# A recurrent layer moved beside its input projection, and another order for the first expert mixes of a SwitchHead kernel

## The chip, the cores and the metric

The kernel runs on one core of one Trainium2 chip. The metric is the device time in microseconds of one execution; of several runs the median is given. A profile of one execution stands beside it.

Engine names as the profile has them: PE is TensorE (matrix multiplication; PEld are its weight loads), ACT is ScalarE, DVE is VectorE, POOL is GpSimd, SP is SyncE, which here only issues transfers.

## The reference

Two blocks follow each other, each with a layer norm ahead of it and a residual addition behind it. The batch B is 2, the length T 2048, the width D 256.

```python
# block 1: a recurrent layer over T
xi = einsum('btd,hd->bth', layernorm(x), Wi) + bi
h[t] = tanh(xi[t] + h[t-1] @ Wh.T + bh)          # h[-1] = 0
x = x + h
# block 2: attention with 8 heads of 64, values and outputs from experts (E = 5, 2 chosen)
q, k = n @ Wq, n @ Wk                            # n = layernorm(x)
wv = topk_mask(n @ Ws, 2) * sigmoid(n @ Ws)      # per token, head and expert
v = einsum('bthe,btek->bhtk', wv, einsum('btd,edk->btek', n, Wv))
attn = softmax(q * scale @ k.T) @ v
out = einsum('bthe,bthk,ekd->btd', topk_mask(n @ Wd, 2), attn, Wo)
x = x + out
```

All numbers are float32.

## The kernel before

**The recurrent layer.** Time is cut into 128 segments of 16 steps (`NCH` = S = 16 steps, NS = P = 128 segments), so that one step of all segments of both batch rows is one operation of 256 columns. Chunk c below is step c of every segment. In the preparation (L274 to L332) each chunk is normalized on POOL (`normalize`, L217), transposed on PE (`turn_in`, L297, 4 transposes into a tile `tp` of the pool `ps_t`), copied by ACT (L299), and multiplied by Wi (`project_in`, L306: for each half mc of the outputs two matmuls, kc = 0 and 1, of 256 columns into a tile px of `ps_xi`). ACT writes px with both biases added to xi (L313). Statistics for the norm come in groups from DVE (`measure`, `stats`, `scales`). The order of PE is written out: the transposes of chunk c + 1, then the projection of chunk c.

The recurrence is run twice. Run "a" starts every segment from zero states at step 3 (SKIP = 3) and gives the last state of each segment (`ends`). Run "b" starts each segment with the state in which run a left the segment ahead of it, and keeps all states (`hs`). At the end `compare` looks whether run b's last states agree with those that it started from; if not, a slow path would run (`slow`). In `step` (L355) each batch row b and each output half mc is a separate matmul pair of 128 columns (L365), an addition of xi on DVE (L372) and a tanh on ACT (L373). For a step without earlier states only a tanh is taken (L359). Beside run b the earlier states are transposed back (L394), added to x and sent out as x1d (`add_back`, L400, L401), and the second norm is started.

**PSUM.** [...] In the attention `ps_s` holds two tiles of two banks for scores, and `ps_o` one bank "o" for output products and one bank "d" for denominators. A bank is given to a new tile when the operations that read its earlier tile are done.

**The attention's main loop (L1154).** A unit is one head with one quarter of the queries (512), 64 units in all. A unit takes U_T = 4 steps T, and each step handles two key tiles t = 2T and 2T + 1, each of 128 x 1024 scores. So unit 0 is T = 0 to 3. In a step the engines get, in this order: the scores of both tiles on PE (`scores`, L638); on ACT a copy p of each tile to SBUF (`stage`, L650); on DVE the running maximum (`largest`, L660, at the end of a unit L663 to L666). ACT and DVE never read one score tile at once: in most steps the odd tile goes first to DVE and then to ACT, the even one first to ACT. At T = 0, 4, 8 and so on both are copied first, the row maximum of the unit just ended is transposed (`turn_max`, L679), reduced (`reduce_max`, L684), and later spread to all rows by PE (`spread_max`, L693, `top` L699). LAG = 6: in step T the tiles 2(T - 5) and 2(T - 5) + 1 get their maximum subtracted (`subtract`, L706; the first two of a unit on DVE, the others on POOL), their exp follows on ACT (L709), and in step T + 1 they are multiplied by the values v (`products`, L719, into bank "o"). POOL then adds pairs of tiles by an accumulating transfer (`fold`, L731), and PE sums them (`sums`, L740, into "d").

Everything else is hung into the steps by hand, in the tables `before` (ahead of the products), `between` (ahead of the odd tile's maximum), `first_behind` and `behind` (at the end of the step); `at(table, T, f, ...)` (L973) appends. Each engine works through its own instructions in the order in which they were issued.

**What of this the change touches.** For the first head and batch row the expert values are made inside T = 0 to 5: `first_experts(c)` (L594) for 16 chunks, three in a step, is 16 PE records (L577) into a bank ("d" for odd c, `misc` for even c) and a copy by ACT (L604) into a tile xf that holds four chunks (a part). After the fourth, SP sends the part to DRAM for later heads (L606). `mix(0, part)` then takes the gates of four chunks (L620, a small copy into a `misc` bank) and multiplies xf by them in place (L622); `mix_sum` (L628) sums over the experts into v. The gates come from `gates` (L959), which POOL finishes (L245 to L256). The output products of T = 6 need part 0 of v, those of T = 7 part 1, and so on. The scheduling is in L996 to L999:

```python
for part in range(4):
    if i == 0:
        at(behind, (3, 5, 6, 7)[part], mix, i, part)
        at(behind, (3, 5, 6, 7)[part], mix_sum, i, part)
```

Of the kernel before, what the change touches and what calls it, by code (L numbers as in the profile page):

```python
# [20 lines left out]
def pass_over(  # L21
# [20 lines left out]
    def tile_pool(name, **kw):  # L42
        return tc_pool(name=name + mark, **kw)
# [80 lines left out]
    def misc(shape, nm):  # L124
        return ps_m.tile(shape, F32, tag="m", name=nm)
# [133 lines left out]

    S = NCH  # L260
    NS = P
    NEWTON = 3


# [8 lines left out]

    with tile_pool(name="prep", bufs=3) as pp, tile_pool(  # L274
        name="lna", bufs=3
    ) as lnp, tile_pool(name="ps_xi", bufs=3, space=PSUM) as ps_xi, tile_pool(
        name="ps_t", bufs=3, space=PSUM
    ) as ps_t, tc.manual_schedule():
        norm_of, turned = {}, {}

        def measure(c0, n):
            mv = pp.tile([P, n * B, 2], F32, tag=f"mv{n}", name=f"mva{c0}")
            for c in range(c0, c0 + n):
                for b in range(B):
                    stats(lnp, mv[:, (c - c0) * B + b, :], xt[c][:, b, :], f"a{c}_{b}")
            neg, y = scales(lnp, mv, n * B, f"a{c0}")
            for c in range(c0, c0 + n):
                norm_of[c] = neg, y, (c - c0) * B

        def turn_in(c):  # L290
            neg, y, k = norm_of.pop(c)
            xn = pp.tile([P, B, D], F32, tag="xn", bufs=2, name=f"xn{c}")
            tp = ps_t.tile([P, KC, B, P], F32, tag="tp", name=f"tpa{c}")
            for b in range(B):
                normalize(xn[:, b, :], xt[c][:, b, :], neg, y, k + b)
                for kc in range(KC):
                    nc.tensor.transpose(tp[:, kc, b, :], xn[:, b, kc * P : (kc + 1) * P], ident)  # L297
            turned[c] = pp.tile([P, KC, B, P], F32, tag="xnT", bufs=2, name=f"xnT{c}")
            nc.scalar.copy(turned[c], tp)  # L299

        def project_in(c):
            xnT = turned.pop(c)
            for mc in range(KC):
                px = ps_xi.tile([P, B, P], F32, tag="px", name=f"px{c}_{mc}")
                for kc in range(KC):
                    nc.tensor.matmul(  # L306
                        px.rearrange("p b n -> p (b n)"),
                        lhsT=wi[:, kc, mc * P : (mc + 1) * P],
                        rhs=xnT[:, kc].rearrange("p b n -> p (b n)"),
                        start=kc == 0,  # L310
                        stop=kc == KC - 1,
                    )
                nc.scalar.activation(xi[:, mc, c], px, AF.Identity, bias=bsum[:, mc : mc + 1])  # L313

        groups, c0 = [], 0
        for n in (1, 1, 2, 3, 4, 5):
            groups.append((c0, n))
            c0 += n
        assert c0 == NCH
        measure(*groups.pop(0))  # L320
        nc.vector.tensor_tensor(bsum, bias[:, 0, :], bias[:, 1, :], ALU.add)
        for c in range(NCH):
            while groups and groups[0][0] <= c + 2:
                measure(*groups.pop(0))
            if c == 0:
                turn_in(0)
            if c < 2:
# [14 lines left out]

    TOL = 4 * 2.0**-23
    GC = NCH // 2
    SKIP = 3
# [6 lines left out]

    def step(nm, s, prev, h, ps_h):  # L355
        for b in range(B):
            if prev is None:
                for mc in range(KC):
                    nc.scalar.activation(h[:, mc, b, :], xi[:, mc, s, b, :], AF.Tanh)  # L359
                continue  # L360
            pre = sp.tile([P, KC, NS], F32, tag=f"pre{b}", name=f"pre{nm}_{s}_{b}")
            for mc in range(KC):
                ph = ps_h.tile([P, NS], F32, tag=f"ph{b}_{mc}", name=f"ph{nm}_{s}_{b}_{mc}")
                for kc in range(KC):
                    nc.tensor.matmul(  # L365
                        ph,
                        lhsT=wh[:, kc, mc * P : (mc + 1) * P],
                        rhs=prev(kc, b),
                        start=kc == 0,
                        stop=kc == KC - 1,  # L370
                    )
# [3 lines left out]
    def run(nm, from_zero, keep_states, ps_h, beside=None):  # L375
        prev = None if from_zero else (lambda kc, b: ends[:, kc, b, 0:NS])
        for s in range(SKIP if from_zero else 0, S):
            if keep_states:
                h = hs[:, :, s]
            elif s == S - 1:  # L380
                h = ends[:, :, :, 1:]
            else:
                h = sp.tile([P, KC, B, NS], F32, tag="h", name=f"h{nm}_{s}")
# [132 lines left out]
    with tile_pool(name="ps_h", bufs=1, space=PSUM) as ps_h:  # L516
        if slow:
            nc.gpsimd.memset(hs[:, :, S - 1], 0.0)
            with tc.For_i(0, NS, 1):
                nc.vector.tensor_copy(ends[:, :, :, 1:], hs[:, :, S - 1])  # L520
                run("c", False, True, ps_h)
# [72 lines left out]
    def first_experts(c):  # L594
# [9 lines left out]
        nc.scalar.copy(xq[:, c % 4], pv.rearrange("p e k -> p k e"))  # L604
        if c % 4 == 3:
# [378 lines left out]
    for i, (b, h) in enumerate(heads):  # L984
# [284 lines left out]
```

## Time and profile before

| | |
|---|---|
| median of 3 runs | 1552.19 us (1551.83 to 1552.85) |
| the profiled execution: time / span | 1552.41 us / 1550.6 us |
| busy: PE / DVE / ACT / POOL | 97% / 84% / 80% / 83% of the span |
| preparation up to run a | to 53.1 us |
| run a (PE L365 pha) | 53.1 to 74.7 us |
| run b and second norm | to 121.5 us |
| main loop, T = 0 at 121.5; T = 9 at | 187.6 us |
| expert values (L577 pvf) | 16 groups, 133.4 to 170.4 us |
| L604 ACT, 128x320 | 16 copies of 427 ns |
| L313 ACT, 128x256 with bias | 32 of 474 ns |
| L622 and L628 DVE, 128x1280 | 1486 ns each |
| transfers L606, 640 KB | 2.9 to 4.1 us from issue to landing |

A line of the profile has the line of the kernel, the engine, the operation, what is written and read, the shape, and a count of records; one float32 matmul leaves two records. In a timeline the first two numbers are start and duration in us; in brackets stands how long the engine was idle just before, and what it waited for. Matmuls are pipelined: a group of records lasts some 0.16 us longer than the distance to the next. In a table of stretches each engine has its busy time and its count of instructions.

### The profile page before, as it was taken

The page shows a single profiled execution, that of the slowest core. Times are in us where ns is not written, and L with a number is a line of the kernel's source. Part 1 is how long each engine was busy: PE and PEld are TensorE (multiplying, and loading weights), DVE is VectorE, ACT ScalarE, POOL GpSimd, SP SyncE. Part 2 cuts the span into 40 slices and gives each one's busy share as a digit, 9 for nine tenths or more (in the row PEclk, how much of TensorE's full clock was granted, in tenths as well). Part 3 has the DMA queues.
Part 4 walks back from the last instruction along what each step waited for, and adds up shares of the span by engine and source line. Part 5 has one row for each costly group of instructions (what it writes and reads, how often), then busy time and mean ns, then how long its engine had stood idle before and what let it go on. Part 6 is the DMA issues. An engine that isn't in the chain of part 4 may idle for free.

```text
span 1550.6 us, 42383 instructions
## 1 busy us (share of the span) xinstructions
PE 1506.5 (97%) x18078; PEld 533.0 (34%) x18078; DVE 1301.1 (84%) x1807; ACT 1242.5 (80%) x1585; POOL 1284.3 (83%) x852
## 2 busy tenths in 40 slices
PE   6999899999999999999999999999999999999997
PEld 5994222222233333333223332222222222222234
DVE  7374899999998888888987778999989999999974
ACT  4674688888888888888887678888888888888872
POOL 3154699999999988999998688899999999999980
PEclk9999999999999999999999999999999999999999
DMA  6021478898888887788797677888888888888965
GB/s 177 1 110 32 116 166 196 188 182 183 181 178 185 185 166 163 169 177 177 165 206 165 166 164 173 173 175 180 176 180 179 175 171 174 174 174 173 208 146 135
DMA packets 87127, 254.52 MB, mean 164 GB/s; under 512 B 11792, under 2 KB 31376, under 8 KB 86928
## 3 DMA queue, kind: packets, MB, share of 16 engines
q0 software_dynamic: 43488, 164.65, 58.0%
q1 hardware_dynamic: 41808, 86.46, 17.0%
q8 instruction: 143, 2.34, 0.6%
q10 hardware_dynamic: 1632, 0.61, 0.2%
q14 instruction: 56, 0.46, 0.1%
HBM read 59.79 MB, written 50.33 MB: 71 GB/s over the span
## 4 chain that ended last, share of the span: by engine, by line
PE 65%; DVE 18%; ACT 7%; issue 5%; DMA 2%; POOL 1%; ACTq 0%; SPq 0%; DVEq 0%; POOLq 0%
PE s L638 22%; PE o L719 18%; DVE m L660 10%; ACT p L650 5%; PE d L740 5%; PE pk L144 3%; PE pq L163 3%; DVE pro L785 3%; PE pz L899 2%; PE phb L365 2%; PE px L306 1%; PE pha L365 1%; DMA p<-p 1%; ACT p L709 1%; PE pv L577 1%
## 5 line engine op out<-in xcount | busy, mean ns | idle before, releaser
L706 POOL TENSOR_TENSOR p<-p,top 128x1024 f32<-128x1024 f32 x378 | 1009.6, 2780 | 26.2 <-ACT top L699 25.9
L650 ACT COPY p<-s 128x1024 f32<-128x1024 f32 x512 | 511.8, 1013 | 143.8 <-issue 59.2
L709 ACT ACTIVATE p<-p 128x1024 f32<-128x1024 f32 x512 | 538.9, 1064 | 49.5 <-DVE p L706 40.5
L638 PE MATMUL s<-q,k 64*32 64x512 f32 x4096 | 501.5, 596 | 4.7 <-ACT p L650 2.4
L638 PE MATMUL s<-qs,k 64*32 64x512 f32 x4096 | 501.5, 596 | 3.4 <-ACT p L650 1.6
L719 PE MATMUL o<-p,v 128*32 128x512 f32 x4096 | 491.6, 597 | 3.2 <-DVE os L756 2.3
L660 DVE TENSOR_TENSOR m<-s,m 128x1024 f32<-128x1024 f32 x320 | 390.9, 1222 | 83.4 <-PE s L638 73.9
L731 POOL DMA_DIRECT2D p<-p x254 | 264.6, 1043 | 94.4 <-issue 40.7
L719 PEld LDWEIGHTS o<-p,v 128*32 128x32 f32 x4096 | 111.8, 109 | 303.8 <-issue 156.6
L638 PEld LDWEIGHTS s<-q,k 64*32 64x32 f32 x4096 | 100.6, 105 | 155.8 <-ACT p L650 59.5
L638 PEld LDWEIGHTS s<-qs,k 64*32 64x32 f32 x4096 | 100.7, 105 | 153.9 <-ACT p L650 58.1
L706 DVE TENSOR_TENSOR p<-p,pt 128x1024 f32<-128x1024 f32 x126 | 152.5, 1210 | 0.0
L740 PE MATMUL d<-p,ones 128*32 128x512 f32 x1032 | 136.8, 592 | 0.7 <-DMA p<-p 0.7
L660 DVE TENSOR_TENSOR m<-s,p 128x1024 f32<-128x1024 f32 x64 | 78.3, 1224 | 47.2 <-ACT p L650 46.2
L785 DVE TENSOR_TENSOR pro<-po,mr 128x1280 f32<-128x1280 f32 (+1 forms) x65 | 95.6, 1471 | 2.6
L622 DVE TENSOR_TENSOR xq<-xq,wp 128x1280 f32<-128x1280 f32 x60 | 89.2, 1487 | 2.1
L628 DVE TENSOR_REDUCE v<-xq 128x256 f32<-128x1280 f32 x60 | 88.5, 1476 | 0.0
L163 PE MATMUL pq<-xn2T,wq 128*32 128x512 f32 x512 | 62.2, 598 | 0.0
L740 PEld LDWEIGHTS d<-p,ones 128*32 128x32 f32 x1032 | 34.1, 110 | 80.2 <-issue 76.9
L144 PE MATMUL pk<-xn2T,wk 128*32 128x512 f32 x512 | 61.5, 598 | 0.0
L835 POOL DMA_DIRECT2D yd<-pro x48 | 60.9, 1268 | 0.0
L400 POOL TENSOR_TENSOR x<-x,hvb 128x512 f32<-128x512 f32 x14 | 17.9, 1275 | 45.8 <-ACT hs L373 34.2
(176 smaller groups left out, 1473.2 us busy)
## 6 DMA issues: line engine op xcount, KB each, us to landing
p<-p POOLq DMA_DIRECT2D x254, 512.0 KB, 5.4
xq<-xvd SPq DMA_DIRECT2D x60, 640.0 KB, 4.6
yd<-pro POOLq DMA_DIRECT2D x48, 640.0 KB, 6.4
qs<-q SPq DMA_DIRECT2D x64, 128.0 KB, 4.4
yd<-pro SPq DMA_DIRECT2D x8, 640.0 KB, 6.3
y<-yd SPq DMA_DIRECT2D x8, 640.0 KB, 6.9
x<-in_x SPq DMA_DIRECT2D x16, 256.0 KB, 6.2
x1d<-x SPq DMA_DIRECT2D x16, 256.0 KB, 2.0
```

The costliest lines, as they stand in the source:

```text
L144: nc.tensor.matmul(pk[at_col : at_col + 32], lhsT=wk[:, kc, h * DH + g : h * DH + g + 32], rhs=xc[:, kc, c0 // 2 : (c0 + HC) // 2, o, :], ...
L163: nc.tensor.matmul(pq[at_col : at_col + 32, :], lhsT=wq[:, kc, h * DH + g : h * DH + g + 32], rhs=xn2T[:, kc, b, n * QB : (n + 1) * QB], s ...
L622: nc.vector.tensor_tensor(xq, xq, wp.unsqueeze(2).to_broadcast([P, 4, DH, E]), ALU.mult)
L638: nc.tensor.matmul(ss[g : g + 32, o, :], lhsT=k_of[i][half, c, g : g + 32], rhs=q_of[i, n][o][half, :], start=True, stop=True, tile_positi ...
L650: nc.scalar.copy(p, ss)
L660: nc.vector.tensor_tensor(m, ss, ring[t - 1] if c == 1 else m, ALU.max)
L706: eng.tensor_tensor(p, p, top.unsqueeze(1).to_broadcast([P, 2, QB]), ALU.subtract)
L709: nc.scalar.activation(ring[t], ring[t], AF.Exp)
L719: nc.tensor.matmul(o_of[u][at_col : at_col + 32, :], lhsT=v_of[i][:, 2 * c + o, g : g + 32], rhs=ring[t][:, o, :], start=c == 0, stop=c == ...
L731: nc.gpsimd.dma_start(out=ring[t], in_=ring.pop(t + 1), accum_op=ALU.add)
L740: nc.tensor.matmul(den_of[u][32 * g : 32 * (g + 1), :], lhsT=ones32, rhs=ring[(t, t1)[g // 2]][:, g % 2, :], start=first, stop=last, tile_ ...
L785: nc.vector.tensor_tensor(dst, po[:, s : s + n, 0:DH].unsqueeze(1).to_broadcast([P, E, n, DH]), mr[:, s : s + n].rearrange("p s e -> p e s ...
```

## The change

Three things are changed, all in `pass_over`.

1. Run a is taken into the preparation. The new `first_run(c)` is called for chunk c - 1 after the projection of chunk c. From step 4 on it multiplies the states of the step before by Wh and accumulates into the px tile that already holds the projection, both batch rows in one matmul of 256 columns; the tanh reads px and adds the biases. For this px tiles have a bank each, six in all, the transposes' tile `tp` moves into the two `misc` banks, and `run` and `step` lose the case of zero states.
2. The expert values of the first head rotate over three banks, `misc`, "o" and "d", instead of two.
3. The mixes of the first head go to T = 2, 4, 5, 6, and their sums to T = 2, 4, 6, 8; mix 1, sum 1 and sum 3 stand in `between`, the others in `behind`.

```diff
-    ) as lnp, tile_pool(name="ps_xi", bufs=3, space=PSUM) as ps_xi, tile_pool(
-        name="ps_t", bufs=3, space=PSUM
-    ) as ps_t, tc.manual_schedule():
-        norm_of, turned = {}, {}
+    ) as lnp, tile_pool(name="ps_xi", bufs=6, space=PSUM) as ps_xi, tc.manual_schedule():
+        norm_of, turned, px_of, h_of = {}, {}, {}, {}
...
-            tp = ps_t.tile([P, KC, B, P], F32, tag="tp", name=f"tpa{c}")
+            tp = misc([P, KC, B, P], f"tpa{c}")
...
         def project_in(c):
             xnT = turned.pop(c)
+            px_of[c] = []
             for mc in range(KC):
-                px = ps_xi.tile([P, B, P], F32, tag="px", name=f"px{c}_{mc}")
+
+                px = ps_xi.tile([P, 512], F32, tag="px", name=f"px{c}_{mc}")[:, : B * P]
...
+                px = px.rearrange("p (b n) -> p b n", b=B)
                 nc.scalar.activation(xi[:, mc, c], px, AF.Identity, bias=bsum[:, mc : mc + 1])
+                px_of[c].append(px)
+
+        def first_run(c):
+
+            pxs, prev = px_of.pop(c), h_of.pop(c - 1, None)
+            if slow or c < SKIP:
+                return
+            h = ends[:, :, :, 1:]
+            if c < S - 1:
+                h = pp.tile([P, KC, B, NS], F32, tag="h", bufs=2, name=f"ha_{c}")
+            for mc, px in enumerate(pxs):
+                for kc in range(KC if prev is not None else 0):
+                    nc.tensor.matmul(
+                        px,
+                        lhsT=wh[:, kc, mc * P : (mc + 1) * P],
+                        rhs=prev[:, kc],
+                        start=False,
+                        stop=kc == KC - 1,
+                        skip_group_check=True,
+                    )
+                nc.scalar.activation(h[:, mc], px, AF.Tanh, bias=bsum[:, mc : mc + 1])
+            h_of[c] = h
...
             if c >= 2:
                 project_in(c)
+            if c:
+                first_run(c - 1)
+        first_run(NCH - 1)
...
-            if prev is None:
-                for mc in range(KC):
-                    nc.scalar.activation(h[:, mc, b, :], xi[:, mc, s, b, :], AF.Tanh)
-                continue
...
-                run("a", True, False, ps_h)
-                run("b", False, True, ps_h, beside)
+                run("b", ps_h, beside)
...
-        pv = ps_o.tile([P, E, DH], F32, tag="d", name=f"pvf{c}") if c % 2 else misc([P, E, DH], f"pvf{c}")
+        tag = (None, "o", "d")[c % 3]
+        pv = ps_o.tile([P, E, DH], F32, tag=tag, name=f"pvf{c}") if tag else misc([P, E, DH], f"pvf{c}")
...
             if i == 0:
-                at(behind, (3, 5, 6, 7)[part], mix, i, part)
-                at(behind, (3, 5, 6, 7)[part], mix_sum, i, part)
+                at(between if part == 1 else behind, (2, 4, 5, 6)[part], mix, i, part)
+                at(between if part % 2 else behind, (2, 4, 6, 8)[part], mix_sum, i, part)
```

More of the change, by code (lines that the diff above doesn't have):

```diff
@@ L261, in pass_over @@
     NS = P
+    SKIP = 3
     NEWTON = 3
@@ L302, in project_in @@
             xnT = turned.pop(c)
+            px_of[c] = []
             for mc in range(KC):
-                px = ps_xi.tile([P, B, P], F32, tag="px", name=f"px{c}_{mc}")
+                px = ps_xi.tile([P, 512], F32, tag="px", name=f"px{c}_{mc}")[:, : B * P]
                 for kc in range(KC):
                     nc.tensor.matmul(
-                        px.rearrange("p b n -> p (b n)"),
+                        px,
                         lhsT=wi[:, kc, mc * P : (mc + 1) * P],
@@ L312, in project_in @@
                     )
+                px = px.rearrange("p (b n) -> p b n", b=B)
                 nc.scalar.activation(xi[:, mc, c], px, AF.Identity, bias=bsum[:, mc : mc + 1])
+                px_of[c].append(px)
[9 more added lines that the diff above has]
+                    nc.tensor.matmul(
+                        px,
+                        lhsT=wh[:, kc, mc * P : (mc + 1) * P],
[6 more added lines that the diff above has]
+            h_of[c] = h
         groups, c0 = [], 0
@@ L332, in pass_over @@
                 project_in(c)
+            if c:
+                first_run(c - 1)
+        first_run(NCH - 1)
     TOL = 4 * 2.0**-23
     GC = NCH // 2
-    SKIP = 3
     sp = rw.enter_context(tile_pool(name="step", bufs=3))
@@ L373, in step, with run @@
                 nc.scalar.activation(h[:, mc, b, :], pre[:, mc, :], AF.Tanh)
[L375 to L383, printed above, removed]
+    def run(nm, ps_h, beside=None):
+        prev = lambda kc, b: ends[:, kc, b, 0:NS]
+        for s in range(S):
+            h = hs[:, :, s]
             step(nm, s, prev, h, ps_h)
@@ L520, in pass_over @@
                 nc.vector.tensor_copy(ends[:, :, :, 1:], hs[:, :, S - 1])
-                run("c", False, True, ps_h)
+                run("c", ps_h)
             for c in range(S):
```

## The prediction

> **What bounds the kernel now.** I read the stages first: the busy time of each engine in stretches that I set by the steps T of the main loop.
>
> ```profile
> core 0: us, PE busy (x) PEld busy (x) DVE busy (x) ACT busy (x) POOL busy (x), PEclk, DMA share, GB/s
> 24.33:53.11 28.78, 27.94 (x151) 24.11 (x151) 11.86 (x58) 19.52 (x40) 11.94 (x22) 1.00 0.05 10
> 53.11:74.65 21.54, 21.54 (x192) 21.54 (x193) 13.68 (x47) 14.81 (x49) 0.00 (x0) 1.00 0.01 2
> 141.80:150.00 8.20, 7.12 (x100) 2.34 (x96) 3.53 (x6) 4.53 (x8) 7.54 (x14) 1.00 0.34 112
> 163.30:170.40 7.10, 5.48 (x92) 1.87 (x92) 5.04 (x6) 4.15 (x6) 4.46 (x2) 1.00 0.23 92
> 180.90:187.60 6.70, 5.01 (x57) 1.75 (x57) 6.35 (x11) 4.98 (x6) 6.62 (x6) 1.00 0.53 131
> 187.60:208.00 20.40, 20.40 (x245) 6.01 (x252) 17.01 (x19) 18.03 (x21) 20.24 (x17) 1.00 0.71 151
> 250.00:400.00 150.00, 149.33 (x1749) 42.45 (x1737) 142.96 (x179) 129.20 (x147) 136.89 (x81) 1.00 0.87 188
> ```
>
> TensorE is the bound nearly everywhere. It is full in the projection (24 to 53) and in the run from zero states (53 to 75), and from 187.6 on it idles under 1%. So a lead that TensorE has at 187.6 should last to the end. Only T = 2 to 8 of the main loop leave it room. The timeline of TensorE shows where (columns: start, duration, idle time before and what ended it).
>
> ```profile
> 146.66 3.44 PE L577 MATMUL pvf<-wv,xn2T 128*32 128x320 f32 x48 [1.08 <-ACT q L173]
> 154.73 1.28 PE L577 MATMUL pvf<-wv,xn2T 128*32 128x320 f32 x16 [0.47 <-ACT xf L604]
> 159.36 0.62 PE L693 MATMUL pt<-ident,mq 128*128 128x128 f32 x4 [0.87 <-DVE mq L684]
> 169.14 1.28 PE L577 MATMUL pvf<-wv,xn2T 128*32 128x320 f32 x16 [1.62 <-ACT xf L604]
> 180.90 0.63 PE L638 MATMUL s<-q,k 64*32 64x512 f32 x4 [1.30 <-ACT p L650]
> 183.38 0.63 PE L679 MATMUL pm<-ident,mm 128*128 128x128 f32 x4 [0.53 <-DVE wp L620]
> 187.02 0.65 PE L693 MATMUL pt<-ident,mq 128*128 128x128 f32 x4 [1.16 <-DVE mq L684]
> ```
>
> These waits are 7.03 us in sum. The first, second and fourth are for a PSUM bank of an expert product; the rest follow VectorE, which does the mixes late (T = 3, 5, 6, 7) and stood still before:
>
> ```profile
> 152.08 1.23 DVE L660 TENSOR_TENSOR m<-s,m 128x1024 f32<-128x1024 f32 x1 [3.96 <-PE s L638]
> 165.33 1.23 DVE L660 TENSOR_TENSOR m<-s,m 128x1024 f32<-128x1024 f32 x1 [4.99 <-PE s L638]
> ```
>
> Last, the timeline where the projection hands over to the run:
>
> ```profile
> 48.73 3.62 PE L306 MATMUL px<-xnT,wi 128*128 128x256 f32 x16
> 52.38 0.47 ACT L313 ACTIVATE xi<-px,bsum 128x256 f32<-128x256 f32 x1 [0.39 <-PE px L306]
> 52.76 0.89 ACT L359 ACTIVATE ha<-xi 128x128 f32<-128x128 f32 x4
> 53.11 17.13 PE L365 MATMUL pha<-ha,wh 128*128 128x128 f32 x151 [0.76 <-ACT ha L359]
> ```
>
> **The run beside the projection.** Before: the chain gives 8 records of px 1.733 us, so the px work is issued by 48.73 + 16 x 0.2166 = 52.20, and run b's first matmul is at 74.65: 22.45 us, of which 192 records take 21.54 (112.2 ns each). After: 12 steps of 8 records of 256 columns, 96 x 0.2166 = 20.79. [...]
>
> Each step needs the tanh of the step before. Its latency: 0.16 drain (a group of 8 lasts 1.89, the next follows after 1.73), 0.03 to ScalarE, 0.474 (L313's form, for L359's 0.30 each), 0.04 back: 0.70. Four transposes (0.44 in the chain) and the next projection (1.73) lie between, 2.17 us: covered. Without them a step would stand 0.70 less 0.43, its first matmul, which needs half the tanh only. That happens once, at step 15: 0.27. Run b then waits 0.70 less 0.22: 0.48. Sum 20.79 + 0.27 + 0.48 = 21.54: **0.9 saved**. ScalarE gets 2 x 0.474 more per chunk, 2.5 us of the 3.9 that TensorE needs, so it hides. The matmul into a bank that ScalarE has read waits for a read that is an iteration old. The 48 additions that VectorE loses (0.29 each) and the transposes' move into two shared banks lie beside TensorE: nothing. Run b's own steps don't change. Bounds for this part: a gain of 1.6 (no waits at the ends) and a loss of 1 (a small wait, 0.15, in each of 12 steps; no row shows one in this pattern).
>
> **Expert values and mixes.** I carried the queues forward with the durations of the rows: scores 1.88, three expert groups 3.37, first copy p 1.2 after the scores start, maximum of the odd tile 2.05 after, mix 0.2 + 1.49, sum 1.49.
> - T = 2: the first product takes the output bank and doesn't wait for the copy of q (1.08, with the restart 1.25). Scores of T = 3 at 148.77 instead of 150.02. Mix 0 and its sum run on VectorE from 148.1 to 151.3, in the 3.96 gap; the gates that it needs were written by 146.9 (L256). The maximum behind them could start at 150.83, so it is 0.46 late.
> - T = 3: no wait for a bank, 154.02 instead of 155.94. Mix 0 is gone from here.
> - T = 4: mix 1 and its sum stand in front of the odd tile's maximum, 157.2 to 160.4. Behind them: that maximum (ends 161.6), then the score bank of T = 5 (needed 162.3), and the last expert product's bank (needed 160.1, free 158.9). Mix 1 overwrites what the transfer of part 1 reads. SP issues it at 153.9; four such landed in 2.9 to 4.1 us, so 156.8 to 158.0: nothing to 0.6 late on VectorE, nothing on TensorE. Scores at 161.36 instead of 163.28.
> - T = 5: the three products follow each other, 163.23 + 3.37: scores of T = 6 at 166.60 instead of 170.35. VectorE: maximum of tile 11 to 164.6, subtraction 0 to 165.8, maximum of tile 10 to 166.9, subtraction 1 to 168.0, mix 2 alone to 169.6.
> - T = 6: scores, keys and output products (1.88 + 1.74 + 1.83) bring TensorE to 172.05 instead of 175.80. VectorE: two maxima to 171.95, sum 2, mix 3 to 175.0; part 3 landed by 172.2 (SP issues it at 168.0).
> - T = 7: the odd maximum ends at 176.2, the copy p behind it frees the score bank at 177.2: scores of T = 8 at 177.26 instead of 180.90. What is late is still VectorE, by mix 3.
> - T = 8: the row maximum comes at 179.8 right after its transposes, as no mix stands ahead of it; its spread follows the output products at 181.5, and T = 9 starts at 182.10 instead of 187.60. Sum 3 stands behind the row maximum, ahead of the odd maximum, whose bank is needed at 183.05 and free at 183.1.
>
> TensorE is 5.5 ahead there. GpSimd isn't. Its first accumulating transfer (175.66) needs the products of T = 6 and comes 3.75 earlier, the second needs exp of tile 3 through the products of T = 7 and comes 3.4 earlier; from then on it is full (20.24 of 20.40 us). The exp of tile 15 starts at 208.07, its subtraction has ended by 206.65: 1.4 of slack. A lead over 3.4 + 1.4 = 4.8 can't pass. Later it has room again (136.89 of 150). **4.8 saved.** Bounds: 5.5 (GpSimd never decides), and 1.25, the first wait alone.
>
> **Sum.** 0.9 + 4.8 = 5.7, from the profiled execution's 1552.41 (span 1550.6 and 1.8 around it): 1546.7; the median of the runs is 0.2 lower: 1546.5.
>
> **Rivals.** (1) GpSimd's pace decides without slack: 0.9 + 3.4 = 4.3, 1547.9. For it: 20.24 of 20.40 busy. Against: it waits for VectorE's comparisons of the gates at 215. (2) The time comes back as other waits, since VectorE does the same work: of 180.9 to 187.6 it was busy 6.35 of 6.70. Then only the first bank's wait and the 0.9 remain: 2.1, 1550.1. Against: the two gaps of 3.96 and 4.99. (3) Slower: mix 1 at T = 4 waits for its transfer, and with it the maximum, the score bank and the expert bank. From a landing later than 158.0 TensorE pays one for one; the whole gain is spent at 163.7, 9.8 us after issue; at 12 us the time is 1554.4. Against: landings of 2.9 to 4.1, and a DMA share of 0.34 and less in these stretches. (4) The tanh isn't covered and each of 11 steps stands 0.27: 3.0 less, 1549.5.
>
> **Chances.** Forecast 0.55 (1545 to 1549), (1) 0.15, (2) and (4) 0.18, (3) and what is like it 0.12, of which about half lies beyond 1555.3. A measurement of this kernel tells about 0.2%, 3.1 us, from no change. Faster: the forecast and two thirds of (1), 0.65; slower by more than that, 0.07; between, 0.28. The range from 1545.0 (0.9 and 5.5 and a little) to 1551.5 leaves out most of (3) and the forecast's edge.
>
> **What would show it.** The last px matmul later than 52.2 by about 17 us but run b's first at 73.3, with one idle of some 0.3 and one of 0.5 us; VectorE's mix at 147 to 151; no TensorE wait for L604; scores of T = 9 about 6.4 earlier in all; exp of tile 15 waiting for GpSimd. I am wrong if idle time in front of L365's new twin comes in every step, if L622 waits for a DMA, or if the lead at T = 9 is gone by 250.

## The result and the profile after

The changed kernel takes 1547.38 us (median of 8 runs, 1546.12 to 1549.05), the kernel before 1552.15 on the same chip: a ratio of 0.9969, interval 0.9958 to 0.998. The forecast was 1546.5, range 1545.0 to 1551.5. Its profiled execution took 1548.75 us (span 1546.9). A later execution of the same kernel, also profiled (`e11_after` below), took 1546.76 (span 1544.9). The largest difference between the two lies at the very start. TensorE's granted clock there, over 24 to 27 us, was 0.53 in the first and 1.00 in the second, so I read the steps from both.

Lines are shifted in the changed kernel: px L307, the new step of run a L328 with its tanh L336, run b L387, expert products L593, mix L637 to L645, scores L655, copy p L667, subtraction L723, exp L726, products L736, fold L748, the closing of a chunk of outputs L791 to L802.

The busy times by stage, first profiled execution (T = 2, 5 and 8 are the third to fifth rows):

```profile
core 0: us, PE busy (x) PEld busy (x) DVE busy (x) ACT busy (x) POOL busy (x), PEclk, DMA share, GB/s
24.36:27.85 3.49, 3.49 (x11) 2.75 (x11) 3.15 (x16) 1.06 (x2) 1.73 (x4) 0.54 0.35 68
27.85:75.09 47.24, 46.54 (x237) 40.35 (x235) 8.83 (x41) 30.05 (x62) 9.77 (x18) 1.00 0.00 1
142.32:149.28 6.96, 6.96 (x101) 2.46 (x97) 4.02 (x8) 4.41 (x8) 6.44 (x12) 1.00 0.37 127
161.79:167.03 5.24, 5.24 (x84) 1.95 (x80) 3.44 (x4) 3.26 (x4) 4.50 (x2) 1.00 0.30 125
177.78:182.68 4.90, 4.90 (x57) 1.74 (x57) 4.39 (x9) 4.90 (x6) 4.82 (x4) 1.00 0.76 193
182.68:203.30 20.62, 20.62 (x245) 5.89 (x252) 17.45 (x19) 18.15 (x22) 20.54 (x18) 1.00 0.67 131
250.00:400.00 150.00, 149.36 (x1756) 42.72 (x1756) 142.95 (x184) 130.42 (x150) 137.26 (x80) 1.00 0.87 185
```

T = 2, 5 and 8 took 8.20, 7.10 and 6.70 us before and take 6.96, 5.24 and 4.90 now, with TensorE full in each. The loss is in the last but one row: GpSimd, 20.54 of 20.62. And one row is new, the first: the granted clock was 0.54 while chunk 3 was projected.

TensorE's timeline at the seam between run a and run b:

```profile
68.78 1.89 PE L307 MATMUL px<-xnT,wi 128*128 128x256 f32 x8
70.51 4.02 PE L328 MATMUL px<-ha,wh 128*128 128x256 f32 x16
75.09 2.05 PE L387 MATMUL phb<-ends,wh 128*128 128x128 f32 x16 [0.56 <-ACT ends L336]
```

The run of L328 lies directly behind the projection of L307, with no idle time until the last step. From VectorE's timeline, the same execution:

```profile
148.82 0.18 DVE L637 COPY wp<-gates_all 128x20 f32<-128x20 f32 x1
149.03 1.49 DVE L639 TENSOR_TENSOR xf<-xf,wp 128x1280 f32<-128x1280 f32 x1
150.55 1.49 DVE L645 TENSOR_REDUCE v<-xf 128x256 f32<-128x1280 f32 x1
...
157.10 0.69 DVE L701 TENSOR_REDUCE mq<-pm 128x4 f32<-128x512 f32 x1 [1.80 <-PE pm L696]
157.70 0.17 DVE L637 COPY wp<-gates_all 128x20 f32<-128x20 f32 x1
157.91 1.49 DVE L639 TENSOR_TENSOR xf<-xf,wp 128x1280 f32<-128x1280 f32 x1
```

Mix 0 fills the gap in which VectorE stood for 3.96 us before. Mix 1 doesn't wait for its transfer, but by little: the trace has it issued at 154.57 and landed at 157.49, and the multiplication that overwrites the tile starts at 157.91.

How far the scores of a step start earlier than before, in us, both counted from the kernel's own T = 0:

| T | forecast | changed kernel | parts 2, 3 | part 2 | part 3 |
|---|---|---|---|---|---|
| 3 | 1.25 | 1.29 | 1.29 | 1.29 | 0 |
| 4 | 1.92 | 1.96 | 1.96 | 1.96 | 0 |
| 5 | 1.92 | 2.03 | 2.02 | 1.21 | -1.02 |
| 6 | 3.75 | 3.86 | 3.86 | 3.04 | -1.02 |
| 7 | 3.75 | 3.86 | 3.86 | 1.70 | -1.02 |
| 8 | 3.64 | 3.66 | 3.67 | 1.21 | -0.32 |
| 9 | 5.50 | 5.46 | 5.46 | 1.21 | 1.48 |
| 13 | - | 5.29 | 5.29 | 1.20 | 1.31 |
| 14 | 4.8 (after tile 15) | 4.35 | 4.33 | 1.22 | -0.55 |
| 24 | 4.8 | 4.34 | 4.35 | 1.21 | -1.37 |

### The profile page after: what moved, and what is told of

The parts are those of the page before. It is cut to its first block, busy times and chain, and to the rows that moved or that the text cites. A ratio compares the mean times of both kernels' runs of the same rounds, so it can differ in the third digit from the quotient of the medians.

```text
span 1546.9 us, 42111 instructions
## 1 busy us (share of the span) xinstructions
PE 1505.9 (97%) x17982; PEld 531.0 (34%) x17982; DVE 1287.2 (83%) x1759; ACT 1238.0 (80%) x1559; POOL 1283.5 (83%) x852
## 3 DMA queue, kind: packets, MB, share of 16 engines
q8 instruction: 143, 2.34, 0.6%
## 4 chain that ended last, share of the span: by engine, by line
PE 66%; DVE 18%; ACT 7%; issue 4%; DMA 1%; POOL 1%; ACTq 0%; DVEq 0%; POOLq 0%
PE s L655 23%; PE o L736 18%; DVE m L677 10%; ACT p L667 5%; PE d L757 4%; PE pq L163 4%; PE pk L144 3%; DVE pro L802 3%; PE pz L916 2%; PE phb L387 2%; PE px L307 2%; DMA p<-p 1%; PE px L328 1%; PE pv L593 1%; ACT p L726 1%
## 5 line engine op out<-in xcount | busy, mean ns | idle before, releaser
L723 POOL TENSOR_TENSOR p<-p,top 128x1024 f32<-128x1024 f32 x378 | 1009.4, 2780 | 24.3 <-ACT top L716 24.0
L667 ACT COPY p<-s 128x1024 f32<-128x1024 f32 x512 | 511.5, 1012 | 143.4 <-issue 59.9
L726 ACT ACTIVATE p<-p 128x1024 f32<-128x1024 f32 x512 | 538.9, 1064 | 50.1 <-DVE p L723 40.7
L655 PE MATMUL s<-q,k 64*32 64x512 f32 x4096 | 501.6, 596 | 4.9 <-ACT p L667 2.5
L655 PE MATMUL s<-qs,k 64*32 64x512 f32 x4096 | 501.7, 596 | 4.3 <-ACT p L667 2.5
L736 PE MATMUL o<-p,v 128*32 128x512 f32 x4096 | 491.6, 597 | 3.2 <-DVE os L773 2.3
L748 POOL DMA_DIRECT2D p<-p x254 | 264.7, 1043 | 91.9 <-issue 40.0
L736 PEld LDWEIGHTS o<-p,v 128*32 128x32 f32 x4096 | 111.8, 109 | 303.7 <-issue 155.9
L655 PEld LDWEIGHTS s<-q,k 64*32 64x32 f32 x4096 | 100.6, 105 | 156.1 <-ACT p L667 59.5
L655 PEld LDWEIGHTS s<-qs,k 64*32 64x32 f32 x4096 | 100.6, 105 | 154.7 <-ACT p L667 60.3
L723 DVE TENSOR_TENSOR p<-p,pt 128x1024 f32<-128x1024 f32 x126 | 152.4, 1210 | 0.0
L802 DVE TENSOR_TENSOR pro<-po,mr 128x1280 f32<-128x1280 f32 (+1 forms) x65 | 95.6, 1471 | 2.6
L645 DVE TENSOR_REDUCE v<-xq 128x256 f32<-128x1280 f32 x60 | 88.6, 1476 | 0.0
L394 DVE TENSOR_TENSOR preb<-phb,xi 128x128 f32<-128x128 f32 x64 | 17.9, 289 | 45.2 <-PE phb L387 45.0
```

The costliest lines, as they stand in the source:

```text
L655: nc.tensor.matmul(ss[g : g + 32, o, :], lhsT=k_of[i][half, c, g : g + 32], rhs=q_of[i, n][o][half, :], start=True, stop=True, tile_positi ...
L667: nc.scalar.copy(p, ss)
L723: eng.tensor_tensor(p, p, top.unsqueeze(1).to_broadcast([P, 2, QB]), ALU.subtract)
L726: nc.scalar.activation(ring[t], ring[t], AF.Exp)
L736: nc.tensor.matmul(o_of[u][at_col : at_col + 32, :], lhsT=v_of[i][:, 2 * c + o, g : g + 32], rhs=ring[t][:, o, :], start=c == 0, stop=c == ...
L748: nc.gpsimd.dma_start(out=ring[t], in_=ring.pop(t + 1), accum_op=ALU.add)
```

## The experiments

My theory after the result had four points. The run beside the projection saves 0.9. The lead at T = 9 needs the banks and the steps together. GpSimd takes back a part, through the output gates and not through the exp that I had named. The spread of the changed kernel's times is the clock at chunk 3. The rivals stand in each expectation. Kernels measured side by side shared a chip and the runs of the kernel before; the ratios are to those. Executions of one kernel lie 4 us apart and more (6.0 in e10_mix1), so a difference of medians under 1 us is read from the traces and not from the medians.

**Each part alone.** `e1_run` has `first_run` and its pools, with the banks and steps of before; `e2_banks_steps` the other two parts; `e3_banks` and `e4_steps` one of these each:

```diff
# e3_banks
-        pv = ps_o.tile(..., tag="d", ...) if c % 2 else misc(...)
+        tag = (None, "o", "d")[c % 3]
+        pv = ps_o.tile(..., tag=tag, ...) if tag else misc(...)
# e4_steps
-                at(behind, (3, 5, 6, 7)[part], mix, i, part)
-                at(behind, (3, 5, 6, 7)[part], mix_sum, i, part)
+                at(between if part == 1 else behind, (2, 4, 5, 6)[part], mix, i, part)
+                at(between if part % 2 else behind, (2, 4, 6, 8)[part], mix_sum, i, part)
```

> Part 1 of the change alone: the run from zero states beside the projection, with the pools and the steps of the mixes as before. Theory: the run takes 96 matmul records of 216.6 ns beside the projection and two waits of about 0.3 and 0.5 us at its end, so from the end of the third chunk's projection to run b's first matmul 47.2 us in place of 48.1: 0.9 us are saved and kept to the end, about 1551.3 us, in executions whose clock holds at 1.0. In executions that take TensorE at half its clock for chunk 3 (the trace of the changed kernel shows 3.49 us for 8 records in place of 1.89), 0.8 slower than that minimum saving allows: about 1552.9. So a median between 1551.3 and 1552.9, and two groups of times some 1.6 to 2.2 us apart. Rival 1: the tanh of one step is not covered, 0.27 us at each of 11 steps: 2.1 us slower than before, 1554.3. Rival 2: nothing is gained, since the attention starts no earlier: 1552.2 in one group.

> Parts 2 and 3 alone: expert values over three banks and the new steps of the mixes, with the run from zero states as its own stage. Theory: the lead of the scores over the kernel before is 5.5 us at T=9 and falls to about 4.3 at T=14, where the closing of the first chunk on VectorE waits for its output gates on GpSimd; it stays there: 4.3 to 5.2 less at the end, about 1547.4 us, and one group of times, since the preparation is that of the kernel before. Rival (the forecast's own cap): the lead after T=15 is 4.8 and nothing on VectorE waits for the gates. Rival 2: the gain needs part 1, lead under 3 us.

> Part 2 alone: expert values over three banks, with the mixes at T=3, 5, 6 and 7 as before. Theory, carried by hand through the first ten chunks: TensorE's waits for the copies of the expert values go, lead of the scores 1.25 us at T=3, 1.9 at T=4 and T=5, 3.75 at T=6, but then the mixes of T=5 to T=7, two steps of VectorE each, stand on the path and give it back: 2.35 at T=7, 1.75 at T=8, 1.5 at T=9; the time is 1.5 us less, about 1550.7. Rival: the lead of T=6, 3.75, holds to the end (the mixes lie beside TensorE): about 1548.4. Rival 2: the banks are worth nothing alone: 1552.2.

> Part 3 alone: the mixes at T=2, 4, 5 and 6 and their sums at T=2, 4, 6 and 8, with the expert values in two banks as before. Theory: TensorE's waits for the copies of the expert values stay, so no lead at T=3 to T=7; VectorE's steps taken apart give 0.75 us at T=8 and 2.6 at T=9, but GpSimd's first folds come no earlier, so that the wait for GpSimd at tile 15 leaves 1.0: about 1551.2 us. Rival: the 2.6 hold to the end, 1549.6. Rival 2: mix 1 a step earlier is late for its transfer, which lands at 157 to 158, and the time rises by 1 or more, 1553.2.

Against the kernel before (1552.50, 40 runs): e1_run 1551.84, ratio 0.9997 (0.9988 to 1.0005). e2_banks_steps 1548.82, 0.9979 (0.9970 to 0.9988). e3_banks 1551.67, 0.9994 (0.9985 to 1.0002). e4_steps 1552.56, 1.0001 (0.9993 to 1.0010).

In the trace of e1_run the start of chunk 3's last px record and run b's first matmul lie 47.62 us apart, in that of before 48.49: 0.87 saved, and the attention behind it is as before to 0.03 us up to T = 40. Its median can't show that. Its times (1550.12 to 1554.43) form no two groups; that part of the expectation failed. e2_banks_steps has the leads of the changed kernel to 0.02 us through T = 24, so up to there part 1 and the others add. Its times were expected in one group near 1547.4, since its preparation is that of before; they lie between 1546.82 and 1550.94, and its trace has the lowered clock at chunk 3 too (0.50 over 26 to 28 us).

Parts 2 and 3 don't add. At T = 14 they have 1.22 and -0.55 alone, together 4.33. With the banks alone, mix 0 with its sum still stands in front of the row maximum, and TensorE's wait for that grows from 0.87 to 1.60, which I hadn't counted when I carried 1.9 for T = 5; the later mixes then hold the copies p. TensorE in e3_banks:

```profile
159.53 0.65 PE L694 MATMUL pt<-ident,mq 128*128 128x128 f32 x4 [1.60 <-DVE mq L685]
175.51 0.63 PE L639 MATMUL s<-qs,k 64*32 64x512 f32 x4 [1.27 <-ACT p L651]
181.11 0.63 PE L639 MATMUL s<-q,k 64*32 64x512 f32 x4 [1.78 <-ACT p L651]
```

With the steps alone both old waits for a bank are there, and a new one between them. TensorE in e4_steps:

```profile
154.67 1.28 PE L577 MATMUL pvf<-wv,xn2T 128*32 128x320 f32 x16 [0.47 <-ACT xf L604]
160.87 3.44 PE L577 MATMUL pvf<-wv,xn2T 128*32 128x320 f32 x48 [1.01 <-DVE xf L622]
170.10 1.28 PE L577 MATMUL pvf<-wv,xn2T 128*32 128x320 f32 x16 [1.62 <-ACT xf L604]
```

The 1.01 is the small copy of gates in front of mix 1. It lies in a `misc` bank, the multiplication on VectorE reads it until 160.82, and the expert product of T = 4 wants that bank. I hadn't counted this tenant, so the lead that I had carried by hand for T = 5, none, was 1.0 off. Over three banks the first product of T = 4 takes bank "o" instead. GpSimd's folds are then 1.0 later as well, the closing of chunk 0 on VectorE waits 1.98 us for its gates, and the lead falls to -0.55 at T = 14, where 1.0 was expected to be left. (The further 0.8 between T = 14 and T = 24 is a stretch at half the clock, from about 214.4 to 217.8 us by the granted clock of 0.80 over 212 to 216 and of 0.77 over 216 to 220. It follows a wait of 1.88 us that TensorE has ahead of T = 14.)

**The fillers.** `e5_fill` puts four unread matmuls into TensorE's idle ahead of chunk 3:

```diff
+            if c == 3:
+                fill = misc([P, 512], "fill")[:, : B * P]
+                for k in range(4):
+                    nc.tensor.matmul(fill, lhsT=wi[:, 0, 0:P], rhs=turned[3][:, 0]..., start=True, stop=True)
             if c + 1 < NCH:
                 turn_in(c + 1)
```

> The changed kernel with four more matmuls of 128x256 on TensorE ahead of chunk 3's projection, which multiply an input already there into a bank that nobody reads, so that TensorE's idle of 1.9 us at 21.5 to 23.5 us is about half filled. They change nothing in what is computed. Theory: the half clock of chunk 3 follows that idle, so the eight records of its projection take 1.9 us in the profiled run (1.5 from the first start to the last) and not 3.5, scores of T=0 start at about 120.5 to 121, and the times lie closer together: the slow half of the changed kernel's executions goes, median some 0.5 to 1 less, about 1546.4. Rival: the granted clock follows its own course, the eight records are at half clock in some executions as before, and the median is that of the changed kernel within 0.5; if the fillers get in the way of chunk 4's transposes, 0.9 slower.

It took 1546.10 us (1545.80 to 1546.99, 5 runs), 0.9964 of before (0.9950 to 0.9977), chunk 3 at full clock (1.00 over 24 to 28 us). For more executions of both I ran the changed kernel and the filled one again side by side:

> The changed kernel itself once more, beside the one with the fillers on the same chip. Theory (the half clock of chunk 3 follows TensorE's idle at 21.5 to 23.5): its executions fall into two groups some 1.6 us apart, as in the first measurement (1546.1 to 1546.7 and 1548.1 to 1549.1), with a third to a half in the upper one. Rival: the spread comes from elsewhere, and it is the same for both kernels.

> The changed kernel with the four fillers once more, beside the changed kernel on the same chip, for more executions of it; the fillers change nothing in what is computed. Theory: no execution has the half clock at chunk 3, so the upper group is missing, the spread is under 1.5 us and the median is 0.5 to 1 below the changed kernel's. Rival: the spread is the changed kernel's, 3 us or more, and the medians agree within 0.4; then the half clock isn't set by that idle.

e11_after 1546.75 (1546.19 to 1549.18, 6 runs), e12_fill 1546.44 (1545.83 to 1547.51, 5 runs), ratios 0.9967 (0.9955 to 0.9979) and 0.9965 (0.9951 to 0.9978). The medians agree within 0.4, as the rival said. The spread with the fillers is 1.7 us, over the 1.5 of the theory and under the 3 of the rival, and of e11_after one execution of six lies in the upper group. Of 14 executions of the changed kernel 5 took over 1548 us, of 10 with the fillers none: with one rate for both that would come out about 1 time in 20. So the times alone don't settle it.

The traces do. Of the 14 profiled executions shown in this document, TensorE stood for 1.9 us ahead of chunk 3's projection in 8, and 4 of these have the lowered clock there (over 26 to 28 us 0.60 in the first execution of the changed kernel, 0.50 in e2_banks_steps, 0.55 in e3_banks, 0.50 in e10_mix1); it stood for 0.6 or less in 6, three with the fillers and three without, and none of these has it (1.00). TensorE at chunk 3 in the first profiled execution of the changed kernel, and then in e11_after:

```profile
23.47 1.10 PE L296 MATMUL tpa<-ident,xn 128*128 128x128 f32 x4 [1.91 <-POOL xn L217]
24.36 3.49 PE L307 MATMUL px<-xnT,wi 128*128 128x256 f32 x8
```

```profile
23.76 0.97 PE L296 MATMUL tpa<-ident,xn 128*128 128x128 f32 x4 [1.91 <-POOL xn L217]
24.57 1.89 PE L307 MATMUL px<-xnT,wi 128*128 128x256 f32 x8
```

The same kernel, and an idle of 1.91 us ahead of these transposes in both; then 3.49 us in one and 1.89 in the other. What differs is when the idle comes. In the first execution the granted clock is recorded at full from 13.94 us, at 0.50 from 24.18, at full again from 27.59 and at 0.50 from 1543.11, behind the last matmul: 3, 4 and 448 times the 3.413 us of that low stretch after the first of these. In the trace of before it is recorded at full from 15.42 us and at 0.50 from 1548.01, behind the last matmul, 449 such stretches later. In e11_after the first rise is recorded at 15.97. At chunk 3 the clock stays low for 3.4 us in all four executions, by its means in windows of 2 us. Laid on stretches of 3.41 us from the first rise, here are the one with the idle and the next in the first execution, and then the two over which the idle falls in e11_after (columns as in the table by stage above):

```profile
20.77:24.18 3.41, 1.40 (x8) 0.74 (x7) 3.00 (x17) 0.91 (x2) 1.32 (x3) 1.00 1.21 205
24.18:27.59 3.41, 3.41 (x10) 2.77 (x10) 3.10 (x16) 1.06 (x2) 1.91 (x4) 0.50 0.42 80
```

```profile
19.38:22.80 3.42, 2.37 (x12) 1.61 (x10) 2.94 (x17) 1.88 (x4) 0.24 (x1) 1.00 1.18 270
22.80:26.21 3.41, 2.36 (x12) 1.94 (x13) 3.21 (x14) 1.06 (x2) 3.06 (x6) 1.00 0.66 120
```

In the first the idle lies in one stretch, of which TensorE was busy for 0.41; in the second it is split, and each half has 0.69. Counted so up to the last matmul, no other stretch of the first execution has less than 0.56, and none of before less than 0.50; before's own idle of 1.91 us is split too (1.72 us busy of the 3.41 from 22.25), and neither trace has another fall of the clock up to there. So in these three executions the lowered clock came where the idle fell into one stretch and not where it was split, and the stretches begin at other times in two executions of the same kernel. For the other executions with this idle that is my reading; it was not shown.

**The output gates.** `e6_gates` makes the output gates of chunks 0 to 7 at T = 3:

```diff
-        at(behind, 7 + 6 * part, gates, 0, part, 1, False)
-        for k in range(E):
-            at(behind, 8 + 6 * part + k, gates_go_on)
+        if part:
+            at(behind, 7 + 6 * part, gates, 0, part, 1, False)
+            for k in range(E):
+                at(behind, 8 + 6 * part + k, gates_go_on)
...
+    at(behind, 3, gates, 0, 0, 1, True)
```

> The changed kernel with the output gates of chunks 0 to 7 made at once at T=3 instead of spread over T=7 to T=12: the same instructions on GpSimd, some 5.5 us of them, ahead of its first subtractions and not between its folds. Theory: GpSimd works without a pause from its first fold at 172 to the end of the gates at 204.6, and that is what the closing of chunk 0 at T=13 waits for; with the gates out of that stretch the closing waits for nothing, and the lead of T=13 (5.3 us, counted from each kernel's own T=0) is kept at T=14 and after, where the changed kernel has 4.35. Some 0.9 us less than the changed kernel at the end. Cost that goes against it: the first subtractions may start 1 us later, at 160.3 in place of 159.2, which has 6 us before the first fold. Rival: the lead after T=14 stays at 4.35, since exp of tile 15 waits for GpSimd's folds and subtractions and not for the gates; then nothing is gained.

1546.24 us (1545.67 to 1548.24, 5 runs), 0.9966 (0.9952 to 0.9979). The lead is 5.30 at T = 13 and still 5.30 at T = 14, 5.34 at T = 24. VectorE at the closing of chunk 0, in the changed kernel and then in e6_gates:

```profile
203.37 0.19 DVE L795 RECIPROCAL po<-den 128x4 f32<-128x4 f32 x1
204.61 0.18 DVE L798 TENSOR_TENSOR mr<-po,gates_all 128x20 f32<-128x20 f32 x1 [1.05 <-POOL gates_all L251]
```

```profile
201.38 0.19 DVE L795 RECIPROCAL po<-den 128x4 f32<-128x4 f32 x1
201.67 0.18 DVE L798 TENSOR_TENSOR mr<-po,gates_all 128x20 f32<-128x20 f32 x1
```

The wait of 1.05 is gone and 0.95 of lead is kept: the theory held. Exp of tile 15, which I had taken for the place, waited 0.17 in the changed kernel (203.61, for GpSimd's L723), and not at all here.

**Mix 3 a step later** (with the gates as in e6_gates): `(2, 4, 5, 6)[part]` becomes `(2, 4, 5, 7)[part]`.

> As the run with the output gates of chunks 0 to 7 made at T=3, and with mix 3 behind T=7 in place of T=6. Theory: at T=8 the scores wait 1.49 us for a copy that VectorE's mix 3 has put off; a step later this lies beside TensorE's work, so the lead grows by 0.5 to 1 us from T=8 on (5.9 to 6.4 at T=9 counted from each kernel's own T=0, where the changed kernel has 5.46) and with the gates out of GpSimd's way it is kept. Rival 1: the mix then stands on the path at T=8 or T=9 and the lead is unchanged at 5.3 by T=10. Rival 2: GpSimd's folds are next, and the lead at T=14 falls back to 4.3.

1546.56 us (1544.43 to 1547.77, 6 runs), 0.9965 (0.9953 to 0.9977). Scores of T = 8 waited for the copy p of T = 7; in the changed kernel and then in e8_mix3:

```profile
177.78 0.63 PE L655 MATMUL s<-q,k 64*32 64x512 f32 x4 [1.49 <-ACT p L667]
```

```profile
175.07 0.63 PE L655 MATMUL s<-q,k 64*32 64x512 f32 x4 [0.57 <-ACT p L667]
```

0.92 less, and the lead is 6.37 at T = 9, 6.21 at T = 14 and 6.23 at T = 24: kept whole up to there. The median doesn't show it, being 0.3 above that of e6_gates.

**Two steps of run a in a row.** In `e7_pairs` first_run is called for two chunks after every second projection:

```diff
-            if c:
+            if c and c % 2 == 0:
+                first_run(c - 2)
                 first_run(c - 1)
+        first_run(NCH - 2)
         first_run(NCH - 1)
```

> The changed kernel with two steps of the run from zero states placed one behind the other after every second chunk's projection, so that in each pair the second step has no projection between it and the tanh it needs. Theory: the tanh of the first of a pair is then in the open, as at the end of the changed kernel's stage, 0.29 us of TensorE idle each time, in 6 to 7 pairs: from the end of chunk 3's projection to run b's first matmul 1.5 to 2 us more than the changed kernel's 47.7 (from start to start), which is more than the 0.87 that the change saved there. Rival: the steps' two halves overlap by themselves and the distance stays at 47.7.

1549.26 us (1547.71 to 1551.65, 20 runs), 0.9982 (0.9976 to 0.9989). From chunk 3's last px to run b 49.86 us instead of 47.61: 2.25 more. TensorE's weight loads show where:

```profile
43.62 1.16 PEld L328 LDWEIGHTS px<-ha,wh 128*128 128x128 f32 x6 [0.51 <-ACT ha L336]
...
51.80 1.16 PEld L328 LDWEIGHTS px<-ha,wh 128*128 128x128 f32 x6 [0.51 <-ACT ha L336]
```

Five pairs (second steps 5, 7, 9, 11, 13) are in the open that were covered, 0.45 us each; I had expected 0.29 in six or seven. The cover was worth more than the whole of part 1.

**Mix 1 a place earlier.** `e10_mix1` brings on the slower rival of the forecast: `at(behind, (2, 3, 5, 6)[part], mix, i, part)`.

> The changed kernel with mix 1 behind T=3, one place ahead of where the change has it. Its values leave for memory at 154.6 and land at 157.5 in the trace of the changed kernel, where the multiplication that overwrites their tile begins at 157.9, 0.4 us later; VectorE is done with the maxima of T=3 at 155.3. Theory (the slower rival of the forecast, brought on by 2.6 us): VectorE waits some 2 us for the transfer, the row maximum mq queued behind it ends 1.9 us later, TensorE waits for it with pt at T=4, and the scores of T=5 start some 1.9 us later than in the changed kernel, counted from T=0; kept to the end, about 1549 us for 1547.4. Rival: the wait lies in VectorE's slack of 1.8 us before mq, and nothing changes.

1550.51 us (1548.24 to 1554.28, 11 runs), 0.9987 (0.9978 to 0.9996). VectorE:

```profile
155.53 0.18 DVE L637 COPY wp<-gates_all 128x20 f32<-128x20 f32 x1
157.81 1.49 DVE L639 TENSOR_TENSOR xf<-xf,wp 128x1280 f32<-128x1280 f32 x1 [2.10 <-DMA xvd<-xf]
159.22 0.68 DVE L701 TENSOR_REDUCE mq<-pm 128x4 f32<-128x512 f32 x1
```

It waits 2.10 us for the transfer, the row maximum queued behind it comes late, and TensorE's `pt` waits 2.7 us for that instead of 0.79. The lead of T = 5 is 0.12, of T = 14 2.41: 1.9 less from there on, as expected. The mechanism of the rival is real, and the change misses it by 0.4 us.

**All that helped together**, `e9_all` (gates, mix 3, fillers):

> The changed kernel with all three: four more matmuls on TensorE ahead of chunk 3's projection (their result is read by nobody), the output gates of chunks 0 to 7 at T=3, and mix 3 behind T=7. Theory: they add up, since each acts at another place: T=0 at about 120.3 with the full clock at chunk 3, 1.9 us more lead at T=14 than the changed kernel; about 1544.3 us, no run with a clock under 0.999, and the times within 1.5 us of each other. Rival: the half clock comes in spite of the fillers, in a third to half of the executions, and the median is near that of the run with the gates and mix 3 alone (1546.6 in the call before, where half its runs were at 0.997).

1545.50 us (1544.97 to 1547.22, 5 runs), 0.9954 (0.9940 to 0.9968). Lead 6.38 at T = 9 and 6.22 at T = 14. That is 1.9 us more than the changed kernel has in the traces, and it holds to T = 121 (6.48, where the changed kernel has 4.49 and 4.61); the intervals of the two ratios still overlap. The expected time was 1.2 lower, and a mean clock of 0.998 in three of its runs was not expected. A part of the 1.9 goes later: at T = 255 the lead is 6.4, and 5.2 and 6.0 in the two executions of the changed kernel. Steps T = 162 and T = 250 last 0.2 us longer in the three traces with the gates moved and in no other, and T = 126 (6.73 in e9_all, 6.00 and 6.58 in the changed kernel) differs from execution to execution.

## Why the prediction was right, step by step

**The run beside the projection, forecast 0.9.** Measured 0.87 or 0.88 in the seven traces that have this stage as the change has it and a full clock. TensorE's chain in the first execution:

```profile
63.33 1.73 PE px L328 x8
65.05 0.44 PE tpa L296 x4
65.49 1.73 PE px L307 x8
67.22 1.73 PE px L328 x8
...
72.44 0.48 ACT ha L336
...
72.96 1.58 PE px L328 x6
...
74.56 0.48 ACT ends L336
...
75.09 0.94 PE phb L387 x6
```

Eight records in 1.73 us, no wait in any step: rival 4 is refuted. The wait at step 15, forecast 0.27, was 0.40: 16 records from 70.67 should have been issued by 70.67 + 16 x 0.2166 = 74.14 and were by 74.54. The wait of run b, forecast 0.48, was 0.55. Together they are 0.2 over the forecast, and yet the total came out, which was luck: the kernel before lost 0.26 at a place that I hadn't counted. In the row below four of its transposes waited between the second and the third and took 0.86 us, where the others take 0.60; in e11_after all of them take 0.60.

```profile
30.71 0.86 PE L297 MATMUL tpa<-ident,xn 128*128 128x128 f32 x4
```

e7_pairs agrees with the larger price, 0.45 for 0.27. My latency of 0.70 was near; what was off is how much of it the first half's matmuls cover.

**TensorE's waits in T = 2 to 8.** The table above: the largest miss is 0.11 us, at T = 5, 6 and 7. The carried queues were right to the place: no wait for a bank is left, and the wait at T = 8 (1.49) is for mix 3. One more wait remains, 0.79 at T = 4 for the row maximum, where before had 0.87.

**"A lead over 3.4 + 1.4 = 4.8 can't pass."** The mechanism held, GpSimd full from its first fold to 204, but both terms were off, and the slack stood at the wrong reader. GpSimd in the changed kernel:

```profile
172.34 1.06 POOL L748 DMA_DIRECT2D p<-p  x1 [6.06 <-ACT p L667]
...
176.01 1.06 POOL L748 DMA_DIRECT2D p<-p  x1
...
198.07 5.51 POOL L723 TENSOR_TENSOR p<-p,top 128x1024 f32<-128x1024 f32 x2
202.79 1.78 POOL L251 TENSOR_SCALAR gates_all<-rank 128x320 f32<-128x320 f32 x1
```

The same in the kernel before, and VectorE at its closing of chunk 0:

```profile
179.33 1.05 POOL L731 DMA_DIRECT2D p<-p  x1
...
201.92 5.19 POOL L706 TENSOR_TENSOR p<-p,top 128x1024 f32<-128x1024 f32 x2
206.65 1.46 POOL L251 TENSOR_SCALAR gates_all<-rank 128x320 f32<-128x320 f32 x1
```

```profile
208.42 0.18 DVE L781 TENSOR_TENSOR mr<-po,gates_all 128x20 f32<-128x20 f32 x1
```

Both folds come 3.86 earlier than before, counted from T = 0 (the second at 179.33 before: 179.33 - 176.01 + 0.54). The gates end at 204.57, before they ended at 208.11, so 4.08 earlier. The closing on VectorE took them up at 208.42 before, 0.31 after their end; in the changed kernel it took them up 0.04 after, so 0.27 of that was slack. 4.08 + 0.27 = 4.35, which is the lead at T = 14. I had looked for the slack only at the exp that I had in mind, and not at each reader of what GpSimd makes in that stretch. The exp's own 1.4 was too long as well: I took the start of the next row (206.65) for the end of the subtractions, which by their own row ran to 201.92 + 5.19 = 207.11. That leaves 0.96, and exp of tile 15 does come 5.0 earlier in the changed kernel (208.07 - 203.61 + 0.54).

**The sum, 5.7.** Of e11_after, at full clock: T = 0 is 0.87 earlier than before, T = 14 is 5.25. Three steps later in the loop (T = 122, 126 and 140) were 0.43, 0.37 and 0.35 shorter than before's. The last addition is 6.9 earlier. The last store then landed 3.94 us after its issue, before 2.98, and the time is 1552.41 - 1546.76 = 5.65 less. So the forecast's 5.7 was met with a smaller gain at T = 14 and two items that I didn't forecast and that nearly cancel: that it came out to 0.05 is luck.

Of the three steps, T = 122 goes with part 1 (5.55 to 5.72 us in the ten traces that have it, 6.04 to 6.77 in the four without), T = 126 lasts 5.50 to 6.82 in no order of the kernels, and T = 140 lasts 7.6 in before and e3_banks and 7.2 in the other twelve. The last store goes with part 1 too. It lands 2.91 to 4.08 us after its issue over the 14 traces, of which the issuing instruction on SyncE makes 1.46 to 1.70 in the four without part 1 and 1.85 to 2.64 in the ten with it, and two executions of one kernel agree (2.34 and 2.51 in the changed kernel, 1.85 and 1.94 with the fillers). So with part 1 the end is later by up to 1.2 us, which can take back the whole 0.87. Why part 1 should change a step and a store so far behind it stays open.

In the first profiled execution chunk 3 at half clock costs 1.6 more (3.49 for 1.89 us), which is most of what separates its 3.66 us from the 5.65. I take it for the reason that the median lies 0.9 over the forecast, between executions near 1546.4 and others near 1548.6; it is shown for this one execution only. (Of the first 8 executions the four over 1548 have a mean clock of 0.997 to 0.998 and the four under it 0.999 to 1.000; in e11_after one of 1546.19 has 0.998 too.) It was no step of mine. The profile of before showed PEclk 1.00 in that stretch.

**The rivals.** GpSimd without slack (1547.9): nearest in size, half right, since the slack was 0.27 and not nil, but on a lead of 4.08. The time coming back as other waits (1550.1): not here, but it is what happens to part 2 or part 3 alone. Slower by the transfer of mix 1: missed by 0.4 us, real in e10_mix1.

## What to carry to other kernels

Where a wait for a bank and a wait for a late engine alternate, fixing one kind hands its gain to the other: parts 2 and 3 gave 1.2 and -0.55 us alone and 4.3 together (at T = 14), so such edits are costed as one carried schedule and not as a sum. When an engine is full, list every reader of what it makes in that stretch with its slack; the tightest one caps the gain (0.27 here, where I took 1.4). A serial chain put behind independent work has its latency hidden only while that work lies between each pair of links (0.45 us per link in the open).

## What the runs showed of the hardware

TensorE's granted clock was 0.53 over 24 to 27 us in the first execution of the changed kernel and 1.00 there in e11_after. At chunk 3 it was lowered, for 3.4 us, in 4 of 14 profiled executions, with part 1 and without it. All four are among the 8 in which TensorE had stood for 1.9 us just before; the other 4 of these and the 6 with an idle of 0.6 us or less had 1.00. In the first execution TensorE was busy for 1.40 of the 3.41 us ahead of the fall. In e11_after the idle fell on two such stretches, busy for 2.37 and 2.36 us, and the clock stayed at 1.00. So the same idle of 1.91 us had either outcome, and what decides between them beyond these executions was not shown. The lowered clock cost 1.6 us (3.49 for 1.89) of a 1550 us kernel, more than the 0.87 that part 1 saves, so an effect of that size has to be read within a trace.
